# The second attention of a two-layer block: context rows as folded queries, one projection after the weighing, interpolation by gathered rows, gate and mix in rows

## The chip, the cores and the metric

The kernel runs on one NeuronCore of a Trainium2 chip. The metric is the time of one execution in device microseconds (us). A core has five engines with a queue each: TensorE (PE in the profile; its weight loads are PEld), VectorE (DVE), ScalarE (ACT), GpSimd (POOL) and SyncE (SP), the last of which only issues transfers here. Each engine takes its instructions strictly in the order of its own queue; engines wait for each other on semaphores. All values are float32.

## The reference, cut to what matters

A block of two layers, each an attention onto the context (1601 rows) and an expert network, runs over 2048 rows `x` of width 256. The change lies in the second layer:

```python
h = layernorm(x)                                      # 2048 x 256
# attention 1: the rows ask the context
c = softmax((h Wq_c + bq_c)(ctx Wk_s + bk_s)^T / 16) (ctx Wv_s + bv_s)      # 2048 x 256
# attention 2: the context asks the rows
s = softmax((ctx Wq_s + bq_s)(h Wk_c + bk_c)^T / 16) (h Wv_c + bv_c)        # 1601 x 256
s = interp_linear(s, 2048)     # row l: two neighbouring rows lo, lo+1, mixed by a share w
g = sigmoid(concat(c, s) Wg^T + bg)
x = x + g * c + (1 - g) * s
# second expert network on layernorm(x); only experts 0 and 1 ever get a weight
```

## The kernel before, in words

The work runs in stages. First comes the first attention; then two shared experts over all rows; then the routed experts: a loop over 39 slots of 128 gathered rows (`up`, `turn`, `down`), which writes its results to a buffer in HBM, `rows_out`. Next each tile of 128 rows gathers two rows per row from `rows_out` with an indirect transfer that POOL issues (L814), adds them into `xs` (L819) and is normed; that stage is called the gather stage here. Then follow the second attention (the context asks) and last the first one of layer 2 (the rows ask) with the gate, the mix and the last expert network.

A softmax is done in transposed form. `scores` (L257) makes tiles `e` with 128 keys in the partitions and up to 512 queries in the columns: matmuls L266, an evacuation by ACT (L270 or L268), a running maximum by DVE (L276 or L274). `shift_exp` (L281) turns that maximum (L288), reduces it (L294), spreads it over the partitions with a diagonal matrix (L296) and a matmul with ones (L302), adds it (L312) and takes the exponential (L315). `weigh` (L320) multiplies `e`, as weights of TensorE, with values of 257 columns, whose last column of ones gives the sum that divides (L327, L834).

Of the second attention, keys and values are projected from the normed rows: `keys` (L232, evacuated at L733) and `values` (L245, L740), block by block of 512 rows in the gather stage. Its queries are the context itself, since the two projections are folded into one matrix. It works in four blocks of context rows (512, 512, 256, 321), and its 1601 result rows stay in SBUF (`sub`). The values of the other attention, from the context, are made inside the routed loop, one tile of context in each of 13 of its rounds.

In the last stage four blocks of 512 rows pass scores, exponential and weighing. After each pair of row tiles, `tail` queues small steps that are taken up between later matmuls: `turn` (the pair is transposed, L220), `interp` (two to four matmuls with a matrix of hats per tile and half, L923, give the interpolated rows in transposed form; POOL makes the difference and the sum, L933 and L935), `gate` (eight matmuls of 256 columns, L944, tanh L948), `back` (transposed again, L957), then `gates` (layernorm, router scores L980) and `mix` (matmuls L1005 of 512 columns, DVE L1011), and the store of the pair.

The order on each engine is not the order of the source: a scheduler places every instruction when the program is built, from its own costs, and from then on the queue of each engine is fixed. A tile of a pool that is used again waits for the readers of what lay there before.

## Time and profile before

| | |
|---|---|
| runs | 1182.01 us median of 3 (1181.16 to 1182.53) |
| profiled execution | 1182.67 us; its span, first to last instruction, 1180.9 us |
| mean granted TensorE clock | 0.967 of full speed |
| busy: PE, DVE, ACT, POOL | 1098.6, 526.5, 345.7, 180.2 us |
| routed loop | 378.0 to 617.6 us |
| gather stage | 617.6 to 698.7 us, PE busy 51.97 us |
| second attention | 698.7 to 880 us |
| last stage | 880 to 1180.9 us, PE busy 280.90 us |

In the profile, a float32 matmul appears as two records and a transpose as one. The duration of a record is longer than the distance between two starts, since matmuls are pipelined; where a row says "24.35 PE mm L327 x112", 112 records followed each other without a gap in 24.35 us. A group row gives busy time, mean time of one instruction, and the idle time of the engine ahead of it with what ended it.

### The profile page before, as it was taken

Reading aid. Unit: us, or ns where it says so; the run is one execution under the profiler, and the core shown is the slowest. Engines: PE = TensorE matmul, PEld = TensorE weight load, DVE = VectorE, ACT = ScalarE, POOL = GpSimd, SP = SyncE. Lnnn points to the kernel's source line nnn. Section 1 sums busy time; section 2 is a strip of 40 time slices with the busy share of each in tenths; the row PEclk is TensorE's granted clock in tenths of the full one; section 3 lists DMA queues with packets and bytes.
Section 4 is the critical chain, followed back from the end, with each engine's and each line's share of the span. In section 5 each row is a group of like instructions: output and inputs, shape, how many; then the busy total and the mean of one; then the engine's idle time right before and its main releaser. Section 6 shows DMA issues by size and latency. Waiting matters only on the chain.

```text
span 1180.9 us, 11717 instructions
## 1 busy us (share of the span) xinstructions
PE 1098.6 (93%) x4043; PEld 701.6 (59%) x4043; DVE 526.5 (45%) x1299; ACT 345.7 (29%) x580; POOL 180.2 (15%) x186
## 2 busy tenths in 40 slices
PE   6997897999999999999994599999999999999985
PEld 3553445665566566666662354588774665757763
DVE  6677889422222222122222725542506646546443
ACT  4752522211110222222212144441405513343110
POOL 1452550033200000000005600000011011110000
PEclk9998898899999999999998799999999999999988
DMA  8410006411103111111102200000000000000000
GB/s 308 144 46 0 1 1 268 168 49 46 40 1 114 45 45 41 41 37 44 46 32 60 84 1 0 1 1 1 18 1 1 1 9 0 9 9 10 9 10 18
DMA packets 34298, 51.91 MB, mean 44 GB/s; under 512 B 5184, under 2 KB 25792, under 8 KB 34240
## 3 DMA queue, kind: packets, MB, share of 16 engines
q1 hardware_dynamic: 24592, 36.74, 9.0%
q0 software_dynamic: 3072, 8.39, 2.2%
q10 hardware_dynamic: 6576, 6.03, 1.5%
q8 instruction: 34, 0.56, 0.2%
q14 instruction: 24, 0.20, 0.1%
HBM read 34.63 MB, written 16.52 MB: 43 GB/s over the span
## 4 chain that ended last, share of the span: by engine, by line
PE 82%; DVE 12%; DMA 3%; ACT 1%; issue 1%; POOL 0%; SPq 0%; POOLq 0%; DVEq 0%; ACTq 0%
PE sc L266 17%; PE mm L327 13%; PE sc L702 11%; PE sc L632 10%; PE mm L722 6%; PE mm L647 5%; PE sc L1005 3%; PE tp L944 2%; PE sc L232 2%; DMA g<-rows_out,slot 2%; PE mm L245 1%; PE tp L714 1%; PE mm L453 1%; DVE st L191 1%; DVE newton L173 1%
## 5 line engine op out<-in xcount | busy, mean ns | idle before, releaser
L702 PE MATMUL sc<-rew,rT 128*128 x312 | 140.3, 592 | 0.6 <-DMA bvs<-in_bvs_dram 0.6
L632 PE MATMUL sc<-hT_f,ew 128*128 128x512 f32 x256 | 116.8, 613 | 0.1
L327 PE MATMUL mm<-vs,e 128*128 128x257 f32 (+1 forms) x416 | 96.9, 380 | 0.0
L702 PEld LDWEIGHTS sc<-rew,rT 128*128 128x128 f32 x312 | 59.0, 190 | 58.8 <-issue 56.8
L315 ACT ACTIVATE e<-e 128x2048 f32<-128x2048 f32 (+3 forms) x48 | 74.3, 1571 | 66.6 <-DVE e L312 65.7
L327 PE MATMUL mm<-vc,e 128*128 128x257 f32 (+1 forms) x416 | 92.3, 379 | 0.0
L312 DVE TENSOR_TENSOR e<-e,tp 128x2048 f32<-128x2048 f32 (+3 forms) x48 | 86.3, 1859 | 13.3 <-PE tp L302 13.3
L266 PE MATMUL sc<-hT,ks 128*128 128x512 f32 (+1 forms) x208 | 91.9, 592 | 0.0
L266 PE MATMUL sc<-ctxT,kc 128*128 128x512 f32 (+2 forms) x256 | 87.2, 499 | 0.0
L327 PEld LDWEIGHTS mm<-vs,e 128*128 128x128 f32 (+1 forms) x416 | 77.3, 190 | 14.0 <-issue 4.0
L327 PEld LDWEIGHTS mm<-vc,e 128*128 128x128 f32 (+1 forms) x416 | 76.8, 185 | 14.9 <-issue 1.9
L708 DVE TENSOR_TENSOR ract<-rsl,sc 128x512 f32<-128x512 f32 x39 | 26.8, 688 | 131.5 <-PE sc L702 128.1
L632 PEld LDWEIGHTS sc<-hT_f,ew 128*128 128x128 f32 x256 | 49.7, 197 | 58.2 <-issue 56.8
L722 PE MATMUL mm<-rew,raT 128*128 x312 | 73.6, 379 | 0.0
L266 PEld LDWEIGHTS sc<-ctxT,kc 128*128 128x128 f32 x256 | 48.4, 189 | 35.7 <-issue 28.8
L266 PEld LDWEIGHTS sc<-hT,ks 128*128 128x128 f32 (+1 forms) x208 | 38.2, 186 | 44.5 <-issue 43.7
L266 PE MATMUL sc<-qT,kT 128*128 128x512 f32 (+1 forms) x104 | 50.4, 641 | 13.5 <-DVE m L274 13.5
L722 PEld LDWEIGHTS mm<-rew,raT 128*128 128x128 f32 x312 | 56.3, 190 | 6.1
L270 ACT ACTIVATE e<-sc,kbc 128x512 f32<-128x512 f32 (+2 forms) x64 | 37.7, 594 | 74.2 <-PE sc L266 74.2
L637 ACT ACTIVATE sl<-sc 128x512 f32<-128x512 f32 x32 | 19.1, 597 | 133.7 <-PE sc L632 133.7
L437 POOL TENSOR_TENSOR acc<-acc,e 128x512 f32<-128x512 f32 (+1 forms) x44 | 57.5, 1307 | 3.4
L270 ACT ACTIVATE e<-sc,kbs 128x512 f32<-128x512 f32 (+1 forms) x52 | 35.5, 685 | 75.5 <-PE sc L266 75.5
(255 smaller groups left out, 1489.2 us busy)
## 6 DMA issues: line engine op xcount, KB each, us to landing
rew<-in_ew_dram SPq DMA_DIRECT2D x24, 512.0 KB, 10.0
rows_in<-zero SPq DMA_DIRECT2D x1, 4992.0 KB, 16.2
rin<-rows_in SPq DMA_DIRECT2D x39, 128.0 KB, 2.0
rows_out<-rout ACTq DMA_DIRECT2D x39, 128.0 KB, 1.7
ew<-in_ew_dram SPq DMA_DIRECT2D x7, 512.0 KB, 8.6
ctxT<-in_ctxT_dram SPq DMA_DIRECT2D x6, 512.0 KB, 7.3
out_dram<-xs SPq DMA_DIRECT2D x8, 256.0 KB, 2.2
xs<-in_x_dram SPq DMA_DIRECT2D x3, 512.0 KB, 5.4
```

The costliest lines, as they stand in the source:

```text
L266: nc.tensor.matmul(ps, kT[:, d, k * P : k * P + r], q[:, d, :], start=(d == 0), stop=(d == nd - 1))
L270: nc.scalar.activation(e[:r, k, :w], ps, AF.Identity, bias=beta[:r, k : k + 1])
L312: nc.vector.tensor_tensor(part, part, bc[:r, :w].unsqueeze(1).to_broadcast([r, k1 - k0, w]), ALU.add)
L315: nc.scalar.activation(part, part, AF.Exp)
L327: nc.tensor.matmul(ov[:c, : D + 1], e[:r, k, j * P : j * P + c], v[:r, k, :], start=(k == 0), stop=(k == len(rows) - 1))
L437: nc.gpsimd.tensor_tensor(acc[:r, :], acc[:r, :], e[:r, k, :], ALU.add)
L632: nc.tensor.matmul(p, w[:, c, cols], hT[:, c, b * BW : (b + 1) * BW], start=(c == 0), stop=(c == DC - 1),)
L647: nc.tensor.matmul(y, act[:, hc, j * P : (j + 1) * P], a2[:, hc, :], start=(hc == 0), stop=(hc == NHC - 1))
L702: nc.tensor.matmul(p, rT[:, c, :], w[:, bass.ds(base + c * HID, HID)], start=(c == 0), stop=(c == DC - 1))
L708: nc.vector.tensor_tensor(act, sl, ps[1], ALU.mult)
L722: nc.tensor.matmul(y, aT[:, hc, :], routed[2][:, bass.ds(base + hc * D, D)], start=(hc == 0), stop=(hc == NHC - 1))
L1005: nc.tensor.matmul(ps, hg[:, c, j * P : (j + 1) * P], ewo[:, c, :, :].rearrange("p x d -> p (x d)"), start=(c == 0), stop=(c == DC - 1),)
```

## The change

The second attention no longer projects the normed rows. The folding is done the other way round, so that the 1601 context rows become queries `qs` of the normed rows themselves (`ctx_rows("c", qs)`); keys are the transposed normed rows `hT`, and values are the normed rows `hr`, without a bias in the scores. The weighing puts `hr` into TensorE as weights and moves `e` through, with the result transposed (`uT`); the sums that divide are made by POOL, which adds the 16 tiles of `e` (`acc`), and a matmul with ones. Only then `out_of` projects each tile of context rows, once, onto 512 columns: 256 of the value and 256 of the value times the second half of the gate's weights (folded in `fold_weights`, biases included). The result goes to a new buffer in HBM, `rows_sub`, 1601 rows of 512 columns.

The interpolation then gathers, for each of 16 row tiles, the lower and the upper neighbours out of `rows_sub` with two indirect transfers, and POOL mixes them (three operations of 128x512) into `sg`. `tail` loses `hats`, `interp` and `back`: the gate multiplies only the transposed pair (first half of the weights) and adds the gathered half; the mix is made in rows. `gates` makes the router scores and the two experts' outputs in one pass of 264 and 256 columns.

Around it: the context's values, its keys and the folding of the expert weights stand after the routed loop instead of within or right behind it; the gather stage has six gather buffers instead of eight, and the scores of the first context block are made there, four tiles after each block of rows; the maximum is spread by transposes instead of a diagonal matrix, in every attention; more weights are loaded by SP ahead of the routed loop.

The scheduler lays the new POOL work of the last stage in this order (from the built program; the three operations of a tile are its subtraction, its scaling and its addition):

```
32 gathers from rows_sub, mixed with the 16 x 3 operations that make sg
8  additions of sg to xs, one per pair of tiles (between the last operations of sg)
8  subtractions that make cdif = rows - sg, one per pair, the first pair's first
```

The first gather waits for all 13 stores to `rows_sub`. In DVE's queue, the product of the first pair, `dif = (z + 1) * dif`, waits for the first of the eight subtractions; behind it stand the layernorm of that pair, the division of the third tile, and all later maxima. In TensorE's queue the transposes of that layernorm's result stand behind the scores of the first two blocks and most of the weighing of the first.

```diff
+    rows_sub = tc.dram_tile([SC, 2 * D], F32, name="rows_sub")
...
-        diag = sp.tile([P, BT, P], F32, name="diag")
...
-            shape = [c, j1 - j0, c]
-            nc.vector.tensor_tensor(
-                diag[:c, j0:j1, :c], ident[:c, :c].unsqueeze(1).to_broadcast(shape),
-                nmx[:c, j0:j1, :].to_broadcast(shape), ALU.mult,
-            )
         yield
-        for c, j0, j1 in pieces:
-            nc.tensor.matmul(
-                bc[:, j0 * P : j0 * P + (j1 - j0) * c].rearrange("p (j q) -> p j q", q=c), ones[:c, :],
-                diag[:c, j0:j1, :c], start=True, stop=True,
-            )
+        for j, c in enumerate(cols):
+            nc.tensor.transpose(bc[:, j * P : j * P + c], nmx[:c, j, :].to_broadcast([c, P]), ident[:c, :c])
...
-        for q, k, n in (("qc", "ks", "s"), ("qs", "kc", "c")):
+        for q, k, n in (("qc", "ks", "s"), ("kc", "qs", "c")):
...
+            wv=load(raw1p, "wvc", [P, DC, D]), bg=load(raw1p, "bg", [P, DC]),
         )
-        return load_ctxT(l1cp)
+        wg = t["wg"]
+        w1["wg1"] = w1pool.tile([P, DC, D], F32, name="wg1")
+        nc.sync.dma_start(w1["wg1"], wg[:, 0:DC, :])
+        w1["wg2"] = raw1p.tile([P, DC, D], F32, name="wg2")
...
-                ones_beside(vs)
-            if 12 <= s < 12 + NCT:
-                values("s", ctxT, s - 12, s - 11, vs, kbs)
-
-        keys(ps_s, "s", ctxT, 0, SC, ks)
-        fold_experts()
...
+        ctx_rows("s", ks)
+        ctx_rows("c", qs)
+        ctx_values()
+        fold_weights()
...
+            h = layernorm(b * BT, BT, prew, hr[:, b * BT : (b + 1) * BT, :])
+            turn_block(ps_t, h, lambda c, tp: copy(c, hT[:, c, b * BW : (b + 1) * BW], tp))
+
+            if b == 0:
+                first_em = score_tiles((eps[0], sp))
+            scores(first_em, hT, S, qs[:, :, 0:BW], BW, None, first=b * BT, end=(b + 1) * BT)
...
+        def out_of(n, lo, w, uT, acc):
+
+            cols = parts_of(w)
+            dps = bank(ps_s)
+            for j, c in enumerate(cols):
+                nc.tensor.matmul(dps[:c, j : j + 1], acc[:, j * P : j * P + c], ones[:, 0:1], start=True, stop=True)
+            rden = sp.tile([P, BT], F32, name="rden4")
+            for c, j0, j1 in [(P, 0, w // P)] + ([(cols[-1], w // P, len(cols))] if w % P else []):
+                nc.vector.reciprocal(rden[:c, j0:j1], dps[:c, j0:j1])
+            for j, c in enumerate(cols):
+                ps = bank(ps_s)
+                for d in range(DC):
+                    nc.tensor.matmul(
+                        ps[:c, :], uT[:, d, j * P : j * P + c], wvg[:, d, :], start=(d == 0), stop=(d == DC - 1)
+                    )
+                r = sp.tile([P, 2 * D], F32, name="sgrow")
+                nc.vector.scalar_tensor_tensor(r[:c, :], ps[:c, :], rden[:c, j : j + 1], bvg[:c, :], ALU.mult, ALU.add)
+                nc.sync.dma_start(rows_sub[lo + j * P : lo + j * P + c, :], r[:c, :])
...
+                def each(r, k0, k1, e=e, acc=acc, w=w):
+                    for k in range(k0, k1):
+                        if k == 1:
+                            nc.gpsimd.tensor_tensor(acc[:, :w], e[:, 0, :w], e[:, 1, :w], ALU.add)
+                        elif k:
+                            nc.gpsimd.tensor_tensor(acc[:, :w], acc[:, :w], e[:, k, :w], ALU.add)
...
-                for j, c in enumerate(parts_of(w)):
-                    ov = weigh(e, vc, S, j, c, between if j == 0 else None)
-                    divided(sub[:c, lo // P + j, :], ov, c, bv["c"])
...
+                for d in range(DC):
+                    ov = bank(ps_m)[:, :w]
+                    for k in range(NT):
+                        if between is not None and d == 0 and k in (3, 8):
+                            next(between)
+                        nc.tensor.matmul(
+                            ov, hr[:, k, d * P : (d + 1) * P], e[:, k, :w], start=(k == 0), stop=(k == NT - 1)
+                        )
+                    nc.scalar.copy(uT[:, d, :w], ov)
+                out_of(blk, lo, w, uT, acc)
...
+        sg = sgp.tile([P, NT, 2 * D], F32, name="sg")
+        for i in range(NT):
+            got = []
+            for k in range(2):
+                g = near.tile([P, 2 * D], F32, name=f"near_rows{k}")
+                nc.gpsimd.indirect_dma_start(
+                    out=g, out_offset=None, in_=rows_sub,
+                    in_offset=bass.IndirectOffsetOnAxis(ap=near_at[k][:, i : i + 1].bitcast(U32), axis=0),
+                    bounds_check=SC - 1,
+                )
+                got.append(g)
+            lo, hi = got
+            nc.gpsimd.tensor_tensor(hi, hi, lo, ALU.subtract)
+            nc.gpsimd.tensor_scalar(hi, hi, share[:, i : i + 1], None, ALU.mult)
+            nc.gpsimd.tensor_tensor(sg[:, i, :], hi, lo, ALU.add)
...
-            def hats():
...
-            def interp():
...
-                            nc.tensor.matmul(
-                                tp[:, (c * 2 + j) * P : (c * 2 + j + 1) * P],
-                                sub[:nr, r, c * P : (c + 1) * P], m[:nr, n, :],
...
+                rows = kept["dif"] = rows_of.pop(i)
+                cT = kept["cT"] = work.tile([P, DC, 2 * P], F32, name="cT")
+                nc.scalar.copy(cT.rearrange("p c q -> p (c q)"), turn_pair(ps_t, rows))
+                xt, s = xs[:, i : i + 2, :], sg[:, i : i + 2, 0:D]
+                nc.gpsimd.tensor_tensor(xt, xt, s, ALU.add)
+                dif = kept["dif"] = work.tile(pair, F32, name="cdif")
+                nc.gpsimd.tensor_tensor(dif, rows, s, ALU.subtract)
...
-                            ps[:, o * W : (o + 1) * W], wg[:, f, o * P : (o + 1) * P], part,
...
-            def back():
...
+                cT, dif = kept["cT"], kept["dif"]
+                ps = bank(ps_t).rearrange("p (j d) -> p j d", d=D)
...
+                            ps[:, j, :], cT[:, c, j * P : (j + 1) * P], wg1[:, c, :], start=(c == 0), stop=(c == DC - 1)
...
+                z = work.tile(pair, F32, name="z")
+                nc.vector.tensor_tensor(z, ps, sg[:, i : i + 2, D : 2 * D], ALU.add)
+                nc.scalar.activation(z, z, AF.Tanh, scale=0.5)
+                nc.vector.scalar_tensor_tensor(dif, z, 1.0, dif, ALU.add, ALU.mult)
+                xt = xs[:, i : i + 2, :]
+                nc.vector.scalar_tensor_tensor(xt, dif, 0.5, xt, ALU.mult, ALU.add)
+
+            return [turn, gate] + gated_experts(i)
...
+                hx = kept["hx"] = fwork.tile([P, 2, NE + 2 * D], F32, name="hx")
+                for j in range(2):
+                    for lo, hi in ((0, D + NE), (D + NE, NE + 2 * D)):
+                        ps = bank(ps_s)[:, : hi - lo]
+                        for c in range(DC):
+                            nc.tensor.matmul(
+                                ps, hg[:, c, j * P : (j + 1) * P], ewg[:, c, lo:hi], start=(c == 0), stop=(c == DC - 1)
+                            )
+                        nc.scalar.copy(hx[:, j, lo:hi], ps)
+                lg = hx[:, :, D : D + NE]
...
-                    ps = bank(ps_s)
-                    for c in range(DC):
-                        nc.tensor.matmul(
-                            ps, hg[:, c, j * P : (j + 1) * P], ewo[:, c, :, :].rearrange("p x d -> p (x d)"),
-                            start=(c == 0), stop=(c == DC - 1),
-                        )
                     xt = xs[:, i + j, :]
-                    for x in range(2):
+                    for x, at in ((0, 0), (1, D + NE)):
                         nc.vector.scalar_tensor_tensor(
-                            xt, ps[:, x * D : (x + 1) * D], sc[:, j, x : x + 1], xt, ALU.mult, ALU.add
+                            xt, hx[:, j, at : at + D], sc[:, j, x : x + 1], xt, ALU.mult, ALU.add
...
```

## The prediction

> **What bounds the kernel now.** I read the busy shares and slices first.
>
> ```profile
> PE 1098.6 (93%) x4043; PEld 701.6 (59%) x4043; DVE 526.5 (45%) x1299; ACT 345.7 (29%) x580; POOL 180.2 (15%) x186
> ...
> PE   6997897999999999999994599999999999999985
> POOL 1452550033200000000005600000011011110000
> PEclk9998898899999999999998799999999999999988
> ```
>
> TensorE is full but for a hole at slices 21 and 22 (the gather stage) and the ends; the clock dips after the hole. The table of stretches says the same by stage:
>
> ```profile
> 378.00:617.60 239.60, 238.45 (x911) 152.01 (x912) 56.24 (x117) 51.75 (x104) 0.13 (x1) 1.00 0.14 42
> 617.60:698.70 81.10, 51.97 (x186) 32.38 (x184) 34.35 (x137) 21.50 (x56) 32.92 (x32) 0.83 0.19 54
> ...
> 726.00:880.00 154.00, 154.00 (x633) 115.99 (x632) 67.85 (x98) 52.86 (x66) 0.98 (x3) 1.00 0.01 4
> 880.00:1181.00 301.00, 280.90 (x1113) 186.85 (x1111) 151.35 (x386) 94.68 (x152) 39.97 (x45) 0.97 0.02 8
> ```
>
> (after the length: PE, PEld, DVE, ACT, POOL busy, clock, DMA). So every matmul removed in loop, second attention and last stage is worth its pitch, until another engine comes to set the pace. The pitch I take from the chain in order of time, where records follow without a gap:
>
> ```profile
> 450.02 1.73 PE mm L722 x8
> ...
> 456.71 1.73 PE mm L722 x8
> ...
> 784.60 13.81 PE sc L266 x64
> ...
> 802.54 24.35 PE mm L327 x112
> ...
> 971.90 1.78 PE tp L923 x16
> ...
> 978.83 1.73 PE tp L944 x8
> ```
>
> Two records make a matmul: 0.432 us for 256 columns (L266 there, L944), 0.435 for 257, 0.858 for 512 (13.73 us for 32 records, L632), 0.537 for 321 (17.28 for 64), 0.22 for 128 (L923), 0.2 for one column (L458, L980); a transpose 0.109. Rounds of the loop with a context tile last 6.69 us (450.02 to 456.71), those without 5.82.
>
> **The change, stage by stage.**
>
> *First stages.* The spreading of the maximum becomes four transposes (0.43 us) for a matmul of 512 columns (0.86). It stands right ahead of the exponential's chain, so four blocks give 1.7 us. The diagonal's DVE operation (0.69 us) is hidden by eight weighing records, 3.44 us: nothing. SP has more to load ahead of the loop: about four issues of 0.4 us more in front of the first rows, which now land 6.7 us after their issue at 367.85 us, some 4 us before TensorE takes them at 378.5; I cost it at 0, at 2 us if the 256 four-byte pieces of one bias are slow.
>
> *Routed loop.* 26 matmuls of 257 columns leave it: 26 x 0.435 = 11.3 us.
>
> *Gather stage.* Read from the timeline, TensorE and POOL:
>
> ```profile
> 656.83 2.10 PE L212 MATMUL tp<-ident,h 128*128 128x128 f32 x8 [21.88 <-DVE h L202]
> 660.84 6.34 PE L232 MATMUL sc<-hT,fold_c 128*128 128x512 f32 x8 [1.91 <-DVE hT L159]
> ...
> 635.71 1.01 POOL L814 DMA_INDIRECT g<-rows_out,slot  x1 [9.74 <-ACT ewo L766]
> 637.03 1.02 POOL L814 DMA_INDIRECT g<-rows_out,slot  x1 [0.30 <-issue]
> ```
>
> The fifth gather waits 9.74 us, since its buffer lies where the expert weights were; in the changed kernel no gather waits for them. The 32 gathers keep a pitch of 1.32 us; six buffers suffice, as 6 x 1.32 = 7.9 us is more than landing (2.8) and addition (0.5). The matmuls moved here (two context projections 22.3, values 11.3, folding some 9, together 43 us from 604.6) fit in that gathering, which ends later, so they cost nothing. In DVE's queue all copies of `hT` now stand behind all four blocks' layernorms. The last of these ended at 681.8; less 1.7, 11.3 and 9.7, and 0.7 for the copy, the first scores start at 659.8, where before they started at 698.7.
>
> *Second attention.* First block: 27.4 us, three waits of 1.9 for transposes and copies, and a cold start after some 12 us of idling. Rule against row: the Trainium skill (TensorE: Matmul & The Clock Gate, Part 1) has the array at half clock for about 3.4 us after idling, a loss of 1.7; the rows L212 and L232 took 8.44 us after the hole and 4.70 in the next block (1.03 and 3.67), a loss of 3.7. I take the row: 36.8 us, to 696.6. The rest: scores 58.5 as before; weighing now 64 x 0.858 + 32 x 0.432 + 32 x 0.537 = 86.0 for 90.3; projection 26 x 0.858 = 22.3; sums 13 x 0.2 = 2.6; transposes 2.8; and 1% for pitch and waits: 174. The stage ends at 871 for 880 (its end is called t0). POOL's sums (15 additions of 1.31 us a block) and ACT's copies lie beside 27 us of matmuls per block: nothing; if the sums came late, each microsecond would count, but even the last block's, done some 19 us after the third block's weighing begins, are asked for only at 35 (13.8 + 4 of projection + 17.3).
>
> *Last stage, TensorE alone.* Off: interpolation 56 x 0.22 = 12.5, half the gate 32 x 0.432 = 13.8, `back` 3.5, router scores 32 x 0.2 = 6.5, spreading 1.7; on: 0.5 for 8 more columns. 301 - 37.5 = 263.5 us. The end of the last pair is about as long: two DVE and one PE step shorter, but the router's chain no longer lies beside 5.5 us of L1005.
>
> *Last stage, the new wait.* POOL's queue holds all of `sg` and all eight additions to `xs` ahead of the first `cdif`. Durations from the groups by form:
>
> ```profile
> L814 POOL DMA_INDIRECT g<-rows_out,slot x32 | 32.9, 1029 | 27.9 <-ACT ewo L766 9.7 <-DMA rows_out<-rout 9.0 <-issue 4.3
> ...
> L933 POOL TENSOR_TENSOR cdif<-cT,sT 128x512 f32<-128x512 f32 x8 | 10.2, 1269 | 236.6 <-ACT sT L929 204.6 <-ACT cT L911 31.9
> ...
> L898 POOL TENSOR_SCALAR pf<-pf 128x256 f32<-128x256 f32 x8 | 6.8, 853 | 0.7
> ```
>
> 32 gathers x 1.32 = 42.2; 32 + 9 two-input operations x 1.27 = 52.1; 16 scalings. No row has a scaling of 512 columns. Below it lies one of 256 (0.85), above it two (1.71); L353, 2.35 us for 1024 columns against 1.27 for 512, puts about 0.19 of a POOL operation in its start, so 0.19 + 2 x 0.66 = 1.52. The skill speaks for less: GPSIMD Engine Reference (3.1 and 4.1) has one-input operations near line rate, 1.03 cycles an element at 1.2 GHz, an estimate of 0.6 us for 512 columns; the row with half the columns already takes more, so I keep 1.52: 24.3, by the page 10. With 0.09 for each of 40 waits of POOL on itself: 122 us, by the page 108. It starts when the last store has landed (scaling 0.75, store about 2.2, as `out_dram`): t0 + 3.1. The first `cdif` is there at t0 + 125; DVE's chain from it to the normed pair took 4.9 us at the end of the kernel before, and has one operation of 0.7 more: t0 + 130.7.
>
> TensorE is at that place after 52 scores of 0.858, 44 weighings, 20 transposes and four gate matmuls: 68 us, with 2% for waits (before: 254 us of work in 259.5) t0 + 69. It stands still for some 62 us. The rest is 164 us of matmuls, 167 with the 2%; 23 for the gaps of the last two pairs and the end (before, 880 to 1180.9 held 20 idle and some 6 cold); 3.7 cold after the stall; 2 while DVE catches up. 130.7 + 167 + 23 + 5.7 = 326.4 us: the stage gives 37 and loses 62.
>
> Sum: 871 + 326.4 = 1197.4 of span, plus 1.8 around it (1182.67 to 1180.9) = 1199. The profiled execution lies 0.7 above the median of the runs, so I predict 1198.5.
>
> **Rivals.** Unknowns of the POOL chain that push up: gathers with rows twice as wide may take POOL longer than 1.32 (1.6 would give 9 us), DVE and POOL may slow each other (POOL's sums took 1.31 where DVE was 76% busy, 1.27 where 50%: 2 us), the scaling may cost 1.71 (3 us), and the gather stage may wait for its six buffers (5 us).
>
> *A slower chain (0.15):* POOL adds 20 us, 1218: the wide gathers at 1.9 us each. Nothing in the profile shows their cost; that a gather's issue lasts 1.03 whether it waits or not speaks against it.
>
> *POOL fast enough (0.10), the other side:* the new chain costs less than the forecast. Break-even lies 16.5 us lower, at a chain of 105 us. The page's price (108) alone gives 1184; with gathers at 1.02 without the 0.30 between, 98 us and 1175. The 1.32 pitch of all gathers and row L898 speak against it.
>
> *No stall (0.03):* if TensorE came to the pair later than POOL, everything saved would stay: 871 + 69 + 167 + 23 + 1.8 = 1132. The chain in order of time has no gap there that could delay TensorE so long.
>
> **How the numbers follow.** Forecast 0.72, its own range 1187 to 1209. About 0.2% (2.4 us) is what a measurement of this kernel tells from no change: faster is below 1179.6, slower above 1184.4. The fast rival lies half there and half in between, no stall is faster, all else slower; of the forecast 0.01 falls in between: faster 0.08, same 0.06, slower 0.86. For 8 in 10 I go from 1183 to 1214.
>
> **What would show it.** Right: one gap of TensorE of 55 to 70 us, some 70 us into the last stage, ahead of a transpose of the layernorm, with DVE idle and POOL without a pause before it; scores of the second attention starting near 660; loop rounds of 5.8 throughout. Wrong: POOL's operations of 512 columns under 1 us; gathers not at 1.3; a gap in the second attention ahead of the sums; a store to `rows_sub` that lands late.

## The result, and the profile after

The changed kernel takes 1190.88 us (median of four runs, 1189.35 to 1192.32), the kernel before beside it 1182.27 us: a ratio of 1.0074 with a 95% interval of 1.0056 to 1.0091. It is slower, by 8.6 us, which is small (0.7%) but clear of the interval. The profiled execution took 1190.47 us, 1188.7 of them span.

First the page of the changed kernel: busy shares and slices.

```profile
PE 1064.5 (90%) x3728; PEld 653.0 (55%) x3728; DVE 519.0 (44%) x1284; ACT 328.4 (28%) x538; POOL 321.3 (27%) x298
...
PE   6997898999999999999997899999999406999994
...
DVE  6687888422222222222236365325146104475654
...
POOL 1461450133200000000056035330379991000000
PEclk9998998899999999999999899999999757999997
```

TensorE has 34 us less to do than before (1064.5 for 1098.6), and a smaller share of the span. The hole of the gather stage (4 and 5 tenths in slices 22 and 23 before, counted from 1) is down to 7 and 8 tenths, and a new hole stands at slices 32 to 34 (29.7 us each). POOL is full in slices 31 to 33 and nearly empty behind them. TensorE's waits from the end of the routed loop on say what the hole waits for (in all, times, longest):

```profile
PE tp L207 <- DVE h L189: 66.7, 8, 53.8
PE sc L255 <- DVE hT L146: 12.6, 4, 11.5
PE tp L207 <- DVE ob L954: 4.1, 3, 2.0
```

One wait of 53.8 us for a layernorm. Around it, in the timelines of TensorE, VectorE and POOL, one fence each:

```profile
929.51 6.69 PE L306 MATMUL mm<-vs,e 128*128 128x257 f32 x30
989.95 0.45 PE L207 MATMUL tp<-ident,h 128*128 128x128 f32 x1 [53.76 <-DVE h L189]
```

```profile
929.78 0.69 DVE L989 TENSOR_TENSOR z<-tp,sg 128x512 f32<-128x512 f32 x1 [5.17 <-PE tp L985]
984.30 0.69 DVE L991 SCALAR_TENSOR_TENSOR cdif<-z,cdif 128x512 f32<-128x512 f32 x1 [53.83 <-POOL cdif L978]
...
989.39 0.73 DVE L189 TENSOR_SCALAR h<-xs,mv,rstd 128x256 f32<-128x256 f32 x2
```

```profile
867.92 1.02 POOL L940 DMA_INDIRECT near_rows<-rows_sub,near  x1 [23.68 <-issue]
...
980.58 2.47 POOL L976 TENSOR_TENSOR xs<-xs,sg 128x512 f32<-128x512 f32 x2
983.01 1.25 POOL L978 TENSOR_TENSOR cdif<-ob,sg 128x512 f32<-128x512 f32 x1
```

VectorE has the gate's `z` at 930.5 and then nothing it may do: the next operation in its queue needs the first `cdif`, which POOL brings 54 us later, as the last thing behind all of `sg` and all eight sums. TensorE stands at the transposes of that pair's `h`.

The table of stretches by stage (length; PE, PEld, DVE, ACT, POOL busy; clock; DMA). The fourth is the last stage up to those transposes:

```profile
375.40:601.90 226.50, 226.50 (x855) 141.92 (x856) 55.37 (x114) 46.11 (x78) 1.82 (x5) 1.00 0.14 44
601.90:656.90 55.00, 43.03 (x169) 28.27 (x167) 32.59 (x134) 19.68 (x53) 32.70 (x32) 0.92 0.27 80
656.90:864.30 207.40, 206.24 (x641) 115.46 (x642) 77.39 (x108) 61.97 (x92) 62.14 (x61) 0.99 0.04 15
864.30:990.00 125.70, 69.97 (x221) 39.97 (x221) 41.57 (x63) 31.01 (x36) 109.44 (x89) 0.79 0.24 70
990.00:1188.70 198.70, 175.08 (x692) 125.96 (x692) 107.38 (x319) 55.74 (x96) 8.88 (x7) 0.95 0.03 11
```

Before, the routed loop ended at 617.6, the second attention's scores began at 698.7, the last stage at 880. So the change is 15.8 us ahead when the last stage begins, and loses all of that and 8 us more there: 324.6 us for 301.

### The profile page after: what moved, and what is told of

Same layout as the page of the kernel before. It is cut to its first block, busy times and chain, and to the rows that moved or that the text cites. A ratio compares the mean times of both kernels' runs of the same rounds, so it can differ in the third digit from the quotient of the medians.

```text
span 1188.7 us, 11199 instructions
## 1 busy us (share of the span) xinstructions
PE 1064.5 (90%) x3728; PEld 653.0 (55%) x3728; DVE 519.0 (44%) x1284; ACT 328.4 (28%) x538; POOL 321.3 (27%) x298
## 4 chain that ended last, share of the span: by engine, by line
PE 67%; DVE 16%; POOL 8%; DMA 4%; issue 3%; ACT 2%; POOLq 0%; DVEq 0%; SPq 0%; ACTq 0%
PE sc L255 14%; PE sc L691 11%; PE sc L614 10%; PE mm L898 7%; PE mm L711 6%; PE mm L629 5%; PE sc L1013 2%; DVE e L291 2%; POOL near_rows L948 2%; POOL near_rows L940 2%; PE sc L860 2%; DMA g<-rows_out,slot 2%; POOL near_rows L947 2%; PE mm L306 1%; PE tp L703 1%
## 5 line engine op out<-in xcount | busy, mean ns | idle before, releaser
L691 PE MATMUL sc<-rew,rT 128*128 x312 | 140.3, 592 | 0.6 <-DMA bvs<-in_bvs_dram 0.6
L255 PE MATMUL sc<-qs,hT 128*128 128x512 f32 (+2 forms) x256 | 90.3, 510 | 12.6 <-DVE hT L146 12.6
L291 DVE TENSOR_TENSOR e<-e,tp 128x2048 f32<-128x2048 f32 (+3 forms) x48 | 86.3, 1860 | 20.4 <-PE tp L284 20.3
L257 ACT COPY e<-sc 128x512 f32<-128x512 f32 (+3 forms) x116 | 61.2, 535 | 113.2 <-PE sc L255 113.1
L691 PEld LDWEIGHTS sc<-rew,rT 128*128 128x128 f32 x312 | 59.1, 190 | 58.7 <-issue 56.8
L255 PE MATMUL sc<-hT,ks 128*128 128x512 f32 (+1 forms) x208 | 90.6, 592 | 0.0
L898 PE MATMUL mm<-e,hr 128*128 128x512 f32 (+2 forms) x256 | 88.0, 499 | 0.0
L306 PEld LDWEIGHTS mm<-vs,e 128*128 128x128 f32 (+1 forms) x416 | 78.8, 194 | 12.9 <-issue 2.5
L263 DVE TENSOR_TENSOR m<-sc,m 128x512 f32<-128x512 f32 (+3 forms) x100 | 62.6, 626 | 49.7 <-ACT e L257 46.9
L255 PEld LDWEIGHTS sc<-qs,hT 128*128 128x128 f32 x256 | 48.9, 193 | 50.3 <-issue 29.0
L898 PEld LDWEIGHTS mm<-e,hr 128*128 128x128 f32 x256 | 48.2, 190 | 35.4 <-issue 28.2
L207 PE MATMUL tp<-ident,h 128*128 128x128 f32 x32 | 7.2, 326 | 66.7 <-DVE h L189 66.7
L255 PEld LDWEIGHTS sc<-hT,ks 128*128 128x128 f32 (+1 forms) x208 | 38.5, 186 | 47.4 <-issue 46.9
L255 PE MATMUL sc<-qT,kT 128*128 128x512 f32 (+1 forms) x104 | 50.7, 641 | 12.6 <-DVE m L263 12.6
L695 ACT ACTIVATE rsl<-sc 128x512 f32<-128x512 f32 x39 | 23.3, 597 | 134.3 <-PE sc L691 134.3
```

Of the source, the lines that this page charges most:

```text
L255: nc.tensor.matmul(ps, kT[:, d, k * P : k * P + r], q[:, d, :], start=(d == 0), stop=(d == nd - 1))
L257: nc.scalar.copy(e[:r, k, :w], ps)
L263: nc.vector.tensor_tensor(m[:r, :w], ps, upto, ALU.max)
L291: nc.vector.tensor_tensor(part, part, bc[:r, :w].unsqueeze(1).to_broadcast([r, k1 - k0, w]), ALU.add)
L306: nc.tensor.matmul(ov[:c, : D + 1], e[:r, k, j * P : j * P + c], v[:r, k, :], start=(k == 0), stop=(k == len(rows) - 1))
L691: nc.tensor.matmul(p, rT[:, c, :], w[:, bass.ds(base + c * HID, HID)], start=(c == 0), stop=(c == DC - 1))
```

## The experiments

All are edits of the changed kernel unless it is said otherwise. They ran on three other chips than the two kernels above; the kernel before took 1188.7 to 1192.1 us there, so times are compared by their ratio to the kernel before on the same chip.

This table gives the lengths of the stages in each profile, in us. Its bounds are starts of records in TensorE's timeline: the first expert matmul of the routed loop (L691), the first context projection behind it (L219), the first scores of the second attention (L255, `qs,hT`), those of the last stage (L255, `hT,ks`; their start is called t0), the first transposes of a pair's `h` in that stage (L207), the end of the span. The kernel before is cut at its own lines in the same places.

| kernel | loop starts | loop | gather stage | second attention | t0 to first `h` | rest |
|---|---|---|---|---|---|---|
| before | 379.8 | 237.8 | 81.1 | 181.2 | 78.6 | 222.4 |
| changed | 375.4 | 226.5 | 55.0 | 207.2 | 125.8 | 198.8 |
| changed, again | 377.8 | 226.5 | 59.8 | 204.9 | 125.8 | 197.1 |
| diagonal back | 377.6 | 226.5 | 59.6 | 204.9 | 125.9 | 197.1 |
| difference and sum on DVE | 376.5 | 226.5 | 61.6 | 204.9 | 77.2 | 208.5 |
| `sg` in three buffers | 376.8 | 226.5 | 60.3 | 204.9 | 72.8 | 219.5 |
| no scaling | 375.7 | 226.5 | 63.5 | 204.9 | 100.1 | 198.0 |
| sum on DVE early | 375.1 | 226.5 | 61.6 | 204.9 | 134.9 | 194.8 |
| gathers alone on POOL | 376.3 | 226.5 | 65.9 | 204.9 | 91.1 | 192.4 |
| blend on DVE | 374.1 | 226.5 | 65.8 | 204.9 | 84.1 | 213.8 |
| paired rows | 375.7 | 226.5 | 61.0 | 215.9 | 107.9 | 197.9 |
| paired rows, and DVE | 374.8 | 226.5 | 60.4 | 216.0 | 81.9 | 197.3 |
| values in the loop | 375.8 | 237.8 | 52.6 | 204.9 | 125.8 | 198.5 |

The theory at the start: the end moves with POOL's chain, because the first `cdif` is queued behind all of `sg`. The rivals: POOL's amount of work is the bound wherever it stands; the wait has another cause (store, landing of the gathers).

### The first `cdif` leaves POOL's queue

```diff
-                nc.gpsimd.tensor_tensor(xt, xt, s, ALU.add)
...
-                nc.gpsimd.tensor_tensor(dif, rows, s, ALU.subtract)
+                nc.vector.tensor_tensor(dif, rows, s, ALU.subtract)
...
                 nc.vector.scalar_tensor_tensor(xt, dif, 0.5, xt, ALU.mult, ALU.add)
+                nc.vector.tensor_tensor(xt, xt, sg[:, i : i + 2, 0:D], ALU.add)
```

> Both users of a pair's interpolated rows leave POOL's queue: the difference is taken by VectorE ahead of the gate, the sum into xs by VectorE behind the gate's last operation; POOL keeps gathers and sg. My theory (TensorE stands still because the first difference is queued behind all of sg on POOL): the wait of 53.8 us goes, since the first pair's sg is complete some 20 us after the store; 1188.7 less 53.8, less about 1 for the cold start behind the wait, plus some 2 for two more operations of 0.69 us in the chain of the last pairs: 1136. Rival A (VectorE takes over as the bound, with 11 us more work): a part comes back as many small waits, 1150 to 1160. Rival B (the wait has another cause, the store or the gathers' landing): 1185 to 1191.

Measured: 1158.70 us, ratio 0.9724 (0.9707 to 0.9740). The wait of 53.8 us is gone, and t0 to `h` falls from 125.8 to 77.2. But 1136 was expected beside 1182, a ratio of 0.961, and the kernel gave 0.972: 13 us are missing. The table has them in the last stage. Without its stall the changed kernel would need 72.0 us to the first `h` (125.8 - 53.8) and 198.8 behind it; this kernel needs 77.2 and 208.5, 14.9 more, of which some 2 were expected. The gather stage is longer too (61.6 for 55.0), but so it is where the changed kernel ran again (59.8) and for the kernel before on another of these chips (90.2 for 81.1, below), so the ratio has that out. Rival A is right in part: the time comes back as small waits.

```profile
PE tp L207 <- DVE h L189: 25.1, 8, 9.1
PE sc L232 <- ACT qs L761: 7.3, 1, 7.3
PE sc L219 <- ACT qs L761: 6.3, 1, 6.3
```

These are waits of TensorE in that kernel. Without its stall the changed kernel would have 12.9 in the first line (66.7 - 53.8). The 12 us more are the waits of the first two pairs, 5.9 and 6.6 us; the longest, 9.1, is that of the last pair, which the changed kernel has as well (7.3). The other two lines are in the gather stage and were not in the changed kernel's first profile at all.

### Same work, same engine, another order

```diff
-        sg = sgp.tile([P, NT, 2 * D], F32, name="sg")
-        for i in range(NT):
+        sgr = sbuf(ph, "b1r", 3, "right")
+        def near_pair(first):
+            sg = sgs[first] = sgr.tile([P, 2, 2 * D], F32, name="sg")
+            for i in range(first, first + 2):
...
+        for i in range(0, 6, 2):
+            near_pair(i)
...
                 nc.vector.scalar_tensor_tensor(xt, dif, 0.5, xt, ALU.mult, ALU.add)
+                near_pair(i + 6)
```

> Every operation stays on its engine and in its number; sg lives in three rotating buffers of a pair each instead of one for all pairs, so that POOL's queue has the first difference behind three to four pairs of sg and not behind eight. My theory (order in POOL's queue, not POOL's amount of work): POOL then has about 58 us ahead of the first difference, which ends near 927, two us ahead of its use; 1136. Rival A (POOL's 116 us of work are the bound wherever they stand, or POOL, now waiting for each pair's rows, falls behind later): 1150 to 1190. Rival B (another cause): 1185 to 1191.

Measured: 1162.94 us, ratio 0.9759 (0.9743 to 0.9776). POOL has as many operations as in the changed kernel, and this is its first `cdif`:

```profile
931.86 1.27 POOL L987 TENSOR_TENSOR cdif<-ob,sg 128x512 f32<-128x512 f32 x1
```

It ended at 933.1 instead of 984.3, and t0 to `h` was 72.8. So it is the order in POOL's queue that costs the 54 us, and not its amount of work. The 1136 were missed all the same: the rest is the longest of all (219.5, 20.7 more than in the changed kernel). POOL's arithmetic now lies beside every pair instead of ahead of the first; that this is what lengthens the rest was not tested on its own in this kernel.

### A shorter chain

```diff
-            nc.gpsimd.tensor_scalar(hi, hi, share[:, i : i + 1], None, ALU.mult)
```

> Leaves out the 16 scalings by the share, so the interpolated rows are not the reference's; POOL's queue is shorter by 16 x 1.57 = 25.1 us and some gaps, all else as in the changed kernel. My theory (the end moves one for one with POOL's chain as long as TensorE waits for it): the wait falls from 53.8 to about 28, the time to 1163, below the kernel before. Rival A (the gathers' landing, with three buffers of each kind, sets POOL's pace): the chain loses only a part, 1170 to 1188. Rival B (another cause): 1185 to 1191.

Measured: 1172.04 us, ratio 0.9835 (0.9814 to 0.9856); 1163 beside 1182 was expected, 0.984. TensorE's longest wait in this kernel (in all, times, longest):

```profile
PE tp L207 <- DVE h L189: 40.9, 8, 28.0
```

28.0 for 53.8: 25.8 us less for 25.1 us of scalings. Against the changed kernel's 1.0074 the ratio falls by 0.024, 28 us (0.024 x 1182), of which 25.8 are the wait; what is between them is within the two intervals. The end follows POOL's chain one for one.

### Sums on VectorE, but early

This is the first experiment with the sum left where the program had it, ahead of the gate.

```diff
-                nc.gpsimd.tensor_tensor(xt, xt, s, ALU.add)
+                nc.vector.tensor_tensor(xt, xt, s, ALU.add)
...
-                nc.gpsimd.tensor_tensor(dif, rows, s, ALU.subtract)
+                nc.vector.tensor_tensor(dif, rows, s, ALU.subtract)
```

> As the first of these kernels, but the sum into xs stays ahead of the gate in the program, so the planner puts seven of the eight sums between the maxima of the first two blocks in VectorE's queue, each behind a POOL result that is some 13.5 us later than that of the one before. My theory (what stands behind a late operation in its queue waits, on whatever engine): VectorE is held until the seventh pair's sg, near 962; the first pair's rows and the exponentials of the second block are behind it, TensorE stands still from about 925 to 970; about 1180. Rival (work off POOL is enough): 1136, as the first kernel.

Measured: 1200.46 us, ratio 1.0078 (1.0062 to 1.0095), as slow as the changed kernel. Some lines of VectorE's timeline:

```profile
888.90 1.74 DVE L976 TENSOR_TENSOR xs<-xs,sg 128x512 f32<-128x512 f32 x1 [8.88 <-POOL sg L949]
...
971.33 0.69 DVE L976 TENSOR_TENSOR xs<-xs,sg 128x512 f32<-128x512 f32 x1 [12.16 <-POOL sg L949]
981.45 0.69 DVE L976 TENSOR_TENSOR xs<-xs,sg 128x512 f32<-128x512 f32 x1 [5.96 <-POOL sg L949]
982.06 7.27 DVE L291 TENSOR_TENSOR e<-e,tp 128x2048 f32<-128x2048 f32 x4
```

The rival falls: moving the work off POOL is not enough. My size was off (1180 beside 1182 was expected): all eight sums, not seven, stand ahead of the second block's exponentials (L291), so VectorE is held to 982 instead of 962. The eight waits are the same POOL chain, taken in another queue.

### The changed kernel again, and one part of it undone

> The changed kernel as it is, on the chip of this call, so that the others stand beside it. In the four runs before, ScalarE's copies of the context projection came 4 to 8 us late three times while the gathers ran, with nothing in the records that they waited for, and the first scores of the second attention came at 664.8 instead of 656.9. If that belongs to the chip or the moment: it is here too, and the kernel before is also some 10 us longer than 1182. If it belongs to the edits: it is not here.

Measured: 1197.12 us beside 1188.72, ratio 1.0077 (1.0049 to 1.0104): the verdict repeats on another chip. ScalarE is late in the gather stage here too:

```profile
631.75 0.69 ACT L761 ACTIVATE qs<-sc,fbias_c 128x512 f32<-128x512 f32 x1 [5.64 <-issue]
641.57 1.10 ACT L761 ACTIVATE qs<-sc,fbias_c 128x512 f32<-128x512 f32 x3 [9.13 <-remote]
```

Neither row names anything on this core that was waited for ("issue" is time without a releaser, "remote" another core or a queue that the profile doesn't know). So it doesn't belong to the edits. In the changed kernel's first profile the same copies followed each other every 1.72 us.

```diff
+        if wide:
+            diag = sp.tile([P, BT, P], F32, name="diag")
+            nc.vector.tensor_tensor(
+                diag, ident.unsqueeze(1).to_broadcast([P, BT, P]), nmx.to_broadcast([P, BT, P]), ALU.mult
+            )
...
-        for j, c in enumerate(cols):
-            nc.tensor.transpose(bc[:, j * P : j * P + c], nmx[:c, j, :].to_broadcast([c, P]), ident[:c, :c])
+            nc.tensor.matmul(bc.rearrange("p (j q) -> p j q", q=P), ones, diag, start=True, stop=True)
```

> One part undone, in the first attention alone: the maximum is spread by a diagonal and one matmul of 512 columns again, not by four transposes. As predicted (0.43 us of TensorE for each of four blocks, VectorE's diagonal hidden): 1.7 us above the changed kernel. Rival (the diagonal, 0.69 us, was on the chain too, since the exponential waits for the reduction, the diagonal and the matmul in turn): 4 x 1.1, 4.4 us above it, which is how much earlier the loop began in the changed kernel's trace.

Measured: ratio 1.0105 (1.0081 to 1.0130) against 1.0077 (1.0049 to 1.0104). The intervals overlap, and the loop starts of the eleven profiles with the four transposes lie between 374.1 and 377.8 (undone: 377.6). By the intervals the part is worth anything from nothing to some 8 us (0.0065 x 1189); 1.7 and 4.4 are not told apart.

### VectorE beside a computing POOL

An edit of the first experiment's kernel; lower rows are gathered straight into `sg`.

```diff
-            lo, hi = got
-            nc.gpsimd.tensor_tensor(hi, hi, lo, ALU.subtract)
-            nc.gpsimd.tensor_scalar(hi, hi, share[:, i : i + 1], None, ALU.mult)
-            nc.gpsimd.tensor_tensor(sg[:, i, :], hi, lo, ALU.add)
```

> As the kernel with difference and sum on VectorE, but leaves out POOL's subtraction, scaling and addition: the interpolated rows are the lower gathered rows, not the reference's; all 32 gathers stay. In that kernel VectorE's chain from the first gated difference to the normed pair took 11.8 us, where the changed kernel, whose VectorE had stood still until POOL was through, took 5.7. Theory (VectorE's operations are held up while POOL computes): the chain is back at 6.5, TensorE's waits for the layernorm fall from 25 to about 14 us, the time is 10 us below that kernel: 1148 where the kernel before takes 1192, ratio 0.963. Rival (the gathers' writes hold VectorE up): the chain stays near 12, the time within 3 us of 1158, ratio 0.972.

Measured: 1158.87 us, ratio 0.9750 (0.9728 to 0.9772). Three operations of the first pair's chain, in VectorE's timeline of the first experiment's kernel and then of this one:

```profile
934.92 1.30 DVE L990 SCALAR_TENSOR_TENSOR cdif<-z,cdif 128x512 f32<-128x512 f32 x1 [0.70 <-ACT z L989]
...
938.70 1.19 DVE L152 TENSOR_SCALAR ve<-mv 128x2 f32<-128x2 f32 x1
...
943.26 3.66 DVE L189 TENSOR_SCALAR h<-xs,mv,rstd 128x256 f32<-128x256 f32 x2
```

```profile
958.36 0.69 DVE L986 SCALAR_TENSOR_TENSOR cdif<-z,cdif 128x512 f32<-128x512 f32 x1 [0.70 <-ACT z L985]
...
961.53 0.17 DVE L152 TENSOR_SCALAR ve<-mv 128x2 f32<-128x2 f32 x1
...
964.16 0.74 DVE L189 TENSOR_SCALAR h<-xs,mv,rstd 128x256 f32<-128x256 f32 x2
```

The chain takes 6.5 us (958.36 to 964.9) for 12.0 (934.92 to 946.9), and TensorE's waits for `h` are 13.4 us in all for 25.1: those of the first two pairs are 0.4 each for 5.9 and 6.6. This alone doesn't clear the gathers, since here the last of them was issued at 918.8, long before the chain. What does is the time at which the long operations of the first experiment's kernel end, beside POOL's rows there:

```profile
938.59 1.27 POOL L947 TENSOR_TENSOR near_rows<-near_rows,near_rows 128x512 f32<-128x512 f32 x1
...
943.95 1.27 POOL L949 TENSOR_TENSOR sg<-near_rows,near_rows 128x512 f32<-128x512 f32 x1
945.17 1.27 POOL L947 TENSOR_TENSOR near_rows<-near_rows,near_rows 128x512 f32<-128x512 f32 x1
```

`ve` ends at 939.89 and POOL's operation at 939.86; the two `h` end at 946.9, POOL's two at 946.4. And in the kernel with the blend on VectorE, below, four gathers are issued between 948.4 and 953.7, within the first pair's chain, with no arithmetic of POOL in it; the same operations are as short there as without gathers:

```profile
950.23 0.17 DVE L152 TENSOR_SCALAR ve<-mv 128x2 f32<-128x2 f32 x1
...
954.80 0.74 DVE L189 TENSOR_SCALAR h<-xs,mv,rstd 128x256 f32<-128x256 f32 x2
```

So it is POOL's arithmetic that holds VectorE up. The Trainium skill has the rule (SBUF — State Buffer, Who interferes with whom): VectorE and GpSimd share a pair of ports, and a VectorE instruction with two SBUF inputs contends with a GpSimd instruction that reads SBUF, and so may a tensor_scalar; one waits until the other is through. The rows agree: `z`, whose first input is in PSUM, keeps its 0.69 us beside POOL's arithmetic. In the first experiment's kernel that is the second pair's `z`, shown here with the POOL row beside it (the first pair's fell beside a gather):

```profile
965.22 0.69 DVE L988 TENSOR_TENSOR z<-tp,sg 128x512 f32<-128x512 f32 x1 [3.70 <-PE tp L984]
```

```profile
964.25 1.28 POOL L949 TENSOR_TENSOR sg<-near_rows,near_rows 128x512 f32<-128x512 f32 x1
```

The time didn't fall (0.963 was expected), because something else came in: with 32 gathers one after another, TensorE, ScalarE and VectorE stood still for a while with no releaser in the records.

```profile
901.83 0.65 PE L284 MATMUL tp<-ident,nmx 128*128 128x128 f32 x4 [2.65 <-issue]
914.12 3.60 PE L306 MATMUL mm<-vs,e 128*128 128x257 f32 x8 [5.64 <-issue]
922.53 2.08 PE L306 MATMUL mm<-vs,e 128*128 128x257 f32 x4 [4.82 <-issue]
```

That is TensorE in this kernel, 13.1 us; the gathers ran from 877.7 to 919.8. Added to the longer gather stage (65.9 for 61.6) it outweighs what the chain gave. Less these 13.1 the last stage is 270.4 us long (91.1 + 192.4 - 13.1), as long as the changed kernel's without its stall (324.6 - 53.8 = 270.8): an estimate, but it says that POOL's arithmetic is what cost the first experiment its 15 us. Where POOL's arithmetic stands between the gathers, as in the changed kernel, no such wait of TensorE was seen in the last stage, nor beside the first 14 gathers in a row of the next kernel.

### Three versions meant to be better

The blend on VectorE, difference and sum there too, `sg` in two buffers of a pair:

```diff
-                nc.gpsimd.tensor_tensor(hi, hi, lo, ALU.subtract)
-                nc.gpsimd.tensor_scalar(hi, hi, share[:, i : i + 1], None, ALU.mult)
-                nc.gpsimd.tensor_tensor(sg[:, i - first, :], hi, lo, ALU.add)
+                nc.vector.tensor_tensor(hi, hi, lo, ALU.subtract)
+                nc.vector.scalar_tensor_tensor(sg[:, i - first, :], hi, share[:, i : i + 1], lo, ALU.mult, ALU.add)
```

> A version meant to be better: POOL only gathers; the blend of two gathered rows is two VectorE operations (subtract, then times share plus lower row; 32 x 0.72 = 23 us more for VectorE), sg in two rotating buffers of a pair, difference and sum on VectorE. Theory (nothing late ahead of the first pair, no computing on POOL beside VectorE): 1145 to 1152 where the kernel before takes 1192, ratio 0.961 to 0.966; up to 5 us of it may go to gathers that VectorE waits for between the maxima of the first block. Rival (VectorE, some 550 us busy, now sets the pace of the last pairs): 1160 to 1170, ratio 0.973 to 0.982.

Measured: 1171.03 us, ratio 0.9841 (0.9813 to 0.9868), behind the first experiment, and slower than theory or rival had it. In VectorE's waits:

```profile
DVE near_rows L953 <- DMA near_rows<-rows_sub,near: 19.9, 16, 2.2
```

With few buffers a pair's gathers are issued only when a pair before has been blended, and VectorE waits for them within the chain of a layernorm. That and the 23 us of its own operations lie in the 213.8 of the rest; two things were changed at once, and their shares are not told apart. More buffers were not tried.

Paired rows: each projected row is stored once more beside the row ahead of it, and one gather brings both neighbours.

```diff
-    rows_sub = tc.dram_tile([SC, 2 * D], F32, name="rows_sub")
+    rows_sub = tc.dram_tile([SC, 4 * D], F32, name="rows_sub")
...
-                nc.sync.dma_start(rows_sub[lo + j * P : lo + j * P + c, :], r[:c, :])
+                nc.sync.dma_start(rows_sub[at : at + c, 0 : 2 * D], r[:c, :])
+                nc.sync.dma_start(rows_sub[at - 1 + skip : at - 1 + c, 2 * D :], r[skip:c, :])
...
-            for k in range(2):
-                g = near.tile([P, 2 * D], F32, name=f"near_rows{k}")
+            g = near.tile([P, 4 * D], F32, name="near_rows")
```

> The changed kernel with each row of the projected result stored twice, once beside the row ahead of it, so that one gather of 4 KB rows brings both neighbours: 16 gathers on POOL for 32, 25 stores on SyncE for 13, all arithmetic and its order as before. My theory (the end follows POOL's chain): 16 gathers of about 1.19 us with their gap leave it, 19 us, and the store that the first gather waits for lands about 1 us later: TensorE's wait falls from 53.8 to about 36, ratio 0.9925 to the kernel before where the changed kernel has 1.0075. Rival (a gather costs POOL by its bytes): no change, 1.0065 to 1.009.

Measured: 1186.42 us, ratio 0.9950 (0.9933 to 0.9966): faster than before, with the stall still in it. POOL's chain went from 116.3 to 97.6 us (883.72 to 981.33), and a gather's issue took 1.06 us in the mean for 1.05 with rows twice as wide, so the rival falls. TensorE's wait fell from 53.8 to 37.4, as expected. The stores cost 11 us of the second attention (215.9 for 204.9) instead of 1:

```profile
PE tp L207 <- DVE h L189: 50.0, 8, 37.4
PE sc L255 <- DVE sgrow L864: 8.6, 1, 8.6
```

The rows of the result lie in two buffers, and each is now held until two stores have landed.

> The same edit on the kernel with difference and sum on VectorE (0.9724), where TensorE hardly waits for POOL any more. What is left there is VectorE held up while POOL computes, for the first two pairs. Theory: POOL is through some 18 us earlier, ahead of the second pair's layernorm, whose wait (6.6 us) mostly goes: 4 to 6 us, ratio 0.967 to 0.969. Rival (POOL's arithmetic, which is as long, only falls on other operations of VectorE): 0.971 to 0.974.

Measured: 1159.86 us, ratio 0.9735 (0.9719 to 0.9752), no better than the first experiment (0.9724). The two sides are in the table. The last stage falls from 285.7 to 279.2, 6.5 us, about what was expected: the second pair's wait is 0.4 us for 6.6, since POOL is through at 970.6, ahead of that pair, but the first pair's is 10.6 for 5.9. The second attention takes 11 us back. More buffers for those rows weren't tried.

### The context's values back in the loop

```diff
-        ctx_values()
...
+            if 12 <= s < 12 + NCT:
+                ctx_value(s - 12)
```

> One part of the change undone: the 26 matmuls of the context's values stand in the routed loop again, not in the gather stage. As predicted, they cost 26 x 0.435 = 11.3 us in the loop and nothing in the gather stage, which is as long as the gathers: loop 237.8 for 226.5, gather stage unchanged at 55 to 60, ratio 1.017. Rival (the gather stage is now as long as its matmuls, 43 us from the loop's end, or ScalarE's late copies are longer with more of them): the gather stage is 5 to 11 us shorter, ratio 1.0075 to 1.013.

Measured: 1197.20 us, ratio 1.0046 (1.0029 to 1.0063), lower than theory or rival had it, and no slower than the changed kernel. The loop has 237.8 again, 11.3 us more, as predicted. But the gather stage is 52.6 where the changed kernel on another chip had 59.8, and other kernels up to 65.9: 7 to 13 us less, so that little or nothing of the loop's gain was left by the first scores. On the first chip, where the changed kernel's TensorE waited 11.5 us for `hT` in that stage, there would be room for them, but this kernel did not run there; where ScalarE comes late, they are paid, in part or in full.

> The kernel before as it is, for its profile on the chip of this call: in the last two calls it took 1189 to 1192 us, 7 to 10 more than beside the changed kernel's first runs. If ScalarE comes late in the gather stage here too: that stage is 88 to 91 us for 81.1, all others within 1 us of the first profile (loop 237.8, second attention and last stage as they were). If not: the 7 to 10 us are spread over all stages.

A single run of the kernel before, on the last of these chips, took 1190.3 us, span 1188.5. Its loop (237.8), its second attention (181.2) and its last stage up to `h` (78.6) are as in its first profile; the gather stage took 90.2 us for 81.1, as expected. So the chips differ in the gather stage, for the kernel before as well (9 us), and hardly elsewhere. What holds the engines up there stays open: both kernels issue 32 gathers one after another in it, as the kernel with gathers alone on POOL does where it stood still, but the same issue went without a wait in the first profiles of both.

## Why the prediction was right

The forecast was 1198.5 us, 1187 to 1209, by one mechanism: 37 us less for TensorE in the last stage, and a stall of 62 us behind POOL's queue. The mechanism is what happened, in the place named (72.1 us into the stage, ahead of `h`, VectorE idle, POOL hardly pausing: 6.0 us in 116.3), and two experiments show that it is the queue's order (0.9759 with all work still on POOL) and POOL's chain one for one (28.0 for 53.8). TensorE's busy time in the last stage fell by 35.9 us (280.90 before, 69.97 + 175.08 now). The time was 7.6 us lower than forecast. By its steps, against the span of 1188.7:

- *First stages, -1.7:* -4.4 in the traces. Undoing the transposes didn't settle how much of it is theirs.
- *Routed loop, -11.3:* 226.5 for 237.8, exactly; 237.8 again with the values back. Where ScalarE came late, the gather stage took most or all of it back.
- *Gather stage, first scores at 659.8:* 656.9, right to 0.2 us when the 2.7 of the first stages are taken off. "So they cost nothing" held on that chip, but not where ScalarE came late.
- *First block, 36.8 us:* 34.3 (the last of its scores ends at 691.2). The cold start was the disputed term: 3.7 by the row, 1.7 by the skill's rule, an estimate. The changed kernel's second attention took 207.2 us with TensorE idle for 11.5 us ahead of it, and 204.9 in each kernel where it wasn't (the two with paired rows apart): 2.3. The granted clock (the last figure but two) says why, in stretches behind the idling:

```profile
656.90:660.90 4.00, 3.96 (x5) 1.85 (x6) 0.00 (x0) 0.15 (x1) 0.00 (x0) 0.50 0.00 0
660.90:661.90 1.00, 1.00 (x3) 0.30 (x2) 0.00 (x0) 0.44 (x1) 0.00 (x0) 0.70 0.00 0
```

  Half clock until about 661.5, 4.6 us, not 3.4: at half speed that loses 2.3. In the kernel before the clock stayed at 0.50 from 656.8 to 665.8, across the wait of 1.91 us between the two rows; so those rows were some 7.4 us of work at half clock, which is their 3.7, and too dear for one start without such a break. The waits for transposes and copies, 1.9 each, were 1.3.
- *The rest of it, 174:* 172.9. So t0 was 864.1 and not 871.
- *POOL's chain, 122 us from t0 + 3.1:* 116.3 from t0 + 3.8. By form:

```profile
L940 POOL DMA_INDIRECT near_rows<-rows_sub,near x32 | 33.4, 1045 | 29.8 <-issue 27.5 <-POOL near_rows L947 1.3 <-DMA near_rows<-rows_sub,near 0.5
L948 POOL TENSOR_SCALAR near_rows<-near_rows,share 128x512 f32<-128x512 f32 x16 | 25.1, 1571 | 0.5
L949 POOL TENSOR_TENSOR sg<-near_rows,near_rows 128x512 f32<-128x512 f32 x16 | 20.3, 1272 | 0.3
L947 POOL TENSOR_TENSOR near_rows<-near_rows,near_rows 128x512 f32<-128x512 f32 x16 | 20.3, 1270 | 0.1
L976 POOL TENSOR_TENSOR xs<-xs,sg 128x512 f32<-128x512 f32 x8 | 9.9, 1254 | 0.0
```

  The operations were sized right: 1.27 and 1.57 (1.52 predicted; the estimate of 0.6 from the skill's page falls). Busy time is 110.3 with the first `cdif`. What was too dear is the time between them: 13.2 us (32 x 0.30 behind gathers, 40 x 0.09) for 6.0, since a gather behind other work starts after 0.16 us instead of 0.30, and what stands behind a gather starts at once.
- *`h` at t0 + 130.7, TensorE there at t0 + 69:* 125.8 and 72.1, a stall of 53.8 and not 62. VectorE's chain took 5.7 us for 5.7.
- *The remainder, 195.7:* 198.8. Its cold start was near: the clock stood at 0.50 from 989.9 to about 996, an estimate of 3.0 us lost for 3.7.

Together: -6.9 to t0, -4.9 in the chain, +3.1 behind it. That the last stage came out within 2 us (324.6 for 326.4) is in part luck, since its two errors have opposite signs. The rival with the page's price (1184) falls, since no operation had that price; the rival of wide gathers falls twice, at 1.05 us for 2 KB and 1.06 for 4 KB. "No stall" at 1132 would have been too good: with the stall taken out, as in the first experiment, the last stage is 285.7 us long and not 259. Some 15 of these 27 us come from VectorE and POOL working side by side, of which the prediction thought as 2 us; the others are the later arrival (3.1) and the longer remainder (198.8 for 190).

## What to carry to other kernels

An operation that is cheap for its engine can cost as much as everything queued ahead of it: before work moves to an engine with time to spare, count the queue up to the first result that somebody waits for, not the engine's busy share. Let the first consumer's data be produced first, pair by pair; one buffer for all pairs lets the planner put every producer ahead of the first use, and a dependency between pairs (a ring of buffers, or a sum placed behind the operation that it may follow) takes that away. When a stall goes, look at which engines now run at the same time: here 15 of the 54 us did not come back (324.6 to 285.7), most of it VectorE held up beside POOL. The fastest of all is the first experiment's kernel, 0.9724 of the kernel before; that with paired rows as well (0.9735) is not told apart from it.

## What the runs showed of the hardware

- POOL's arithmetic holds VectorE up: a chain of 6.5 us takes 12.0; `ve` took 1.19 us for 0.17, two `h` 3.66 for 0.74. An operation with one input in PSUM kept its 0.69 us, and gathers alone held none of these up.
- A POOL scaling of 128x512 by a value for each partition takes 1.57 us, more than an addition of two such tiles (1.27).
- A gather's issue costs POOL 1.03, 1.05 and 1.06 us in the mean with rows of 1, 2 and 4 KB. It starts 0.30 us behind another gather and 0.16 behind other work.
- With 32 gathers one after another, other engines stood still for up to 11 us at a time with no releaser in the records, on three chips and not on another. The cause is open.
- TensorE's start after 11.5 us of idling cost 2.3 us: the granted clock was 0.50 for some 4.6 us.
